# Layer 0 of a four-layer graph network: from one scatter and one sum to four parts with a running maximum

## The chip, the cores and the metric

The kernel runs on one core of one Trainium2 chip. The metric is the device time of one execution in microseconds (us). A core has five engines that run their own instruction queues and meet at semaphores: PE (matrix products), DVE (vector), ACT (scalar functions), POOL (GpSimd) and SP (it issues transfers here). PEld is PE's weight load, "SPq" the sequencer of SP.

## The reference, cut to what matters

Four graph layers run one after the other on 6250 nodes with 128 features and 100000 edges. Each takes the layer-normalized nodes and adds its result to `x`. Only layer 0 is touched:

```python
h = jnp.maximum(_layernorm(x, axis=-1), 0.0)
# layer 0
h = h @ W_w + W_b
e = h[row] @ a_src + h[col] @ a_dst + a_b
e = jax.nn.leaky_relu(e, negative_slope=0.01)
attention = jax.nn.softmax(e, axis=0)            # over all edges
out = jax.ops.segment_sum(attention * h[col], row, num_segments=6250)
x = x + out
```

The softmax runs over all edges at once, so it needs one maximum and one sum over 100000 values; the segment sum goes by the source node `row`.

## The kernel before, in words

`tile_gnn_stack` first prepares tables that all layers share: for instance the masks `mk_d` in device memory that say, for chunks of edges in order of their target, which edge belongs to which node. It counts how many edges have their source in each of the 49 tiles of 128 nodes (`pc`, `cnt`, L209 to L224). Together with other tests on the edge list this makes a flag; where every tile has at most `CAP` = 2304 edges, and at least `FEW` = 1792 (the last tile 1408), the program takes the fast path.

`attention_sum` (L1083) is layer 0 on that path. Its stages run one after the other:

- **Clear.** `rows_d` in device memory has 2304 rows of 130 numbers for each node tile: a message of 128 numbers, the edge's logit and the edge's source node within its tile. L1105 writes, in two transfers, a neutral row (logit -BIG) into each place from `FEW` up, which a scatter may leave empty.
- **Node table.** `ln_relu` and `transposed` make the normalized nodes and their transpose. A loop over 49 tiles of nodes multiplies by the layer's weights (L1152), adds the bias on DVE (`ev`, four buffers, L1154), stores the tile to the table `T0` with a transfer of SP (L1155) and keeps the source part of the logit in `s_tab` (L1156).
- **Scatter.** A loop over `CH` = 196 chunks of 512 edges. `load` brings masks and node windows for four chunks (SP, three buffers). `look_up(k)` builds one-hot matrices on DVE (L1190 to L1194) and lets PE count each edge's place among its tile's rows (L1198 to L1202), look up the source part of the logit (L1208) and the target node's row (`ph`, L1212). `send(k-1)` picks the place (`sel`, `got`, `pos`, L1223 to L1228), copies the row to `rw` on ACT (L1231, six buffers), adds logit and source (L1233 to L1242), and POOL issues four scatters of 128 rows of 520 bytes (L1161).
- **Sum.** Each of 49 reads brings 2304 rows of a node tile (L1265, 18 rows for each partition); every read waits for all scatters. The maximum and the sum of the exponentials go over the partitions on POOL (L1279, L1284). `total(b)` makes, 18 times for each tile, a one-hot matrix weighted with the exponentials on DVE (`oq`, L1294) and a product on PE (L1296). `next_tables(b)` adds to `x`, takes the next layer's norm (`layer_norm`, L1070 to L1078, with Sqrt on ACT beside the Exp of `total`), transposes, multiplies by layer 1's weights and stores the table `T1` (L1310).

Layer 1 (`mean_layer`) then begins: POOL gathers rows of `T1` (L266) and so needs all of it.

A scheduler sets the order of the instructions within each engine's queue from the program and its dependences; the program's order is a wish. In the queues of the kernel before, SP issues the clear, the small loads, 49 stores of `T0` and then the first mask loads.

Of the kernel before, what the change touches and what calls it, by code (L numbers as in the profile page):

```python
# [17 lines left out]
P = 128  # L18
# [21 lines left out]
CAP = 2304  # L40
FEW = (1792, 1408)
RW = D + 2

# [39 lines left out]
def tile_gnn_stack(ctx: ExitStack, tc: tile.TileContext, a: dict, out: bass.AP):  # L83
# [33 lines left out]
    with ExitStack() as st:  # L117
# [30 lines left out]
        ext = one.tile([P, 6], F32, name="ext")  # L148
# [57 lines left out]
        cp = one.tile([P, 8, NT], F32, name="cp")  # L206
        pc = ps.tile([P, 8, NT], F32, name="pc", bufs=1)
        for g in range(TC // 8):
            oh = work.tile([P, 8, NT], BF, name="oh")  # L209
            V.tensor_tensor(oh, iof[:, None, :NT].to_broadcast([P, 8, NT]),  # L210
                            hi[:, 8 * g:8 * g + 8][:, :, None].to_broadcast([P, 8, NT]),
                            OP.is_equal)
            nc.tensor.matmul(pc, ones_b, oh, start=g == 0, stop=g == TC // 8 - 1)
        V.tensor_copy(cp, pc)
        cnt = one.tile([P, NT], F32, name="cnt")
        V.tensor_reduce(cnt, cp.rearrange("p j b -> p b j"), AX.X, OP.add)
        V.tensor_reduce(ext[:, 4:5], cnt, AX.X, OP.max)
        V.tensor_scalar(ext[:, 4:5], ext[:, 4:5], float(CAP), None, op0=OP.is_gt)
        V.tensor_reduce(ext[:, 5:6], cnt[:, :NT - 1], AX.X, OP.min)
        V.tensor_scalar(ext[:, 5:6], ext[:, 5:6], float(FEW[0]), None, op0=OP.is_lt)  # L220
        V.tensor_scalar(cnt[:, NT - 1:], cnt[:, NT - 1:], float(FEW[1]), None, op0=OP.is_lt)
        V.tensor_tensor(ext[:, 5:6], ext[:, 5:6], cnt[:, NT - 1:], OP.add)
# [5 lines left out]
    far = nc.values_load(flag[0:1, 0:1], min_val=0, max_val=7 * P)  # L228
# [854 lines left out]
def attention_sum(ctx, tc, a, x, hT, T1, sh, ln_relu, transposed, bcast_row):  # L1083
# [13 lines left out]
    rows_d = dram.tile([NT * CAP, RW], F32, name="rows_d")  # L1097
    T0 = dram.tile([NP, D + 1], F32, name="T0")

    none = one.tile([P, 7, RW], F32, name="none")  # L1100
    V.memset(none, 0.0)
    V.memset(none[:, :, D:D + 1], -BIG)
    for b0, nb, few in ((0, NT - 1, FEW[0]), (NT - 1, 1, FEW[1])):
        n = (CAP - few) // P
        nc.sync.dma_start(bass.AP(tensor=rows_d.tensor, offset=rows_d.offset + (b0 * CAP + few) * RW,  # L1105
                                  ap=[[n * RW, P], [CAP * RW, nb], [1, n * RW]]),
                          none[:, None, :n, :].rearrange("p o n f -> p o (n f)")
                          .to_broadcast([P, nb, n * RW]))
    sloE = one.tile([P, TC], F32, name="sloE")
    shiE = one.tile([P, TC], F32, name="shiE")  # L1110
    tile_of(nc, one, srcE, shiE)
    lo = one.tile([P, TC], I32, name="lo")
    V.tensor_scalar(lo, srcE, P - 1, None, op0=OP.bitwise_and)
    V.tensor_copy(sloE, lo)
    eE = one.tile([P, TC], F32, name="eE")
    V.memset(eE[:, TR:], -BIG)
# [6 lines left out]
    base = one.tile([P, NT], F32, name="base")  # L1123
    V.memset(base, 0.0)
    nc.gpsimd.iota(base[0:1, :], pattern=[[CAP, NT]], base=0, channel_multiplier=0,
                   allow_small_or_imprecise_dtypes=True)
# [31 lines left out]
    members = []  # L1158

    def scatter(idx, src):  # L1160
        ins = nc.gpsimd.indirect_dma_start(  # L1161
            out=rows_d, out_offset=bass.IndirectOffsetOnAxis(ap=idx, axis=0), in_=src,
            in_offset=None)
        tc.declare_no_dep(ins.ins, group="rows", reason="each edge has a row of its own")
        tc.add_to_no_dep_group("rows", ins.ins)
        members.append(ins)

    with ExitStack() as se:
        w = se.enter_context(tc.tile_pool(name="s0w", bufs=3))
        gp = se.enter_context(tc.tile_pool(name="s0g", bufs=4))  # L1170
        ps = se.enter_context(tc.tile_pool(name="s0p", bufs=2, space=PSUM))
        masks, live = {}, {}
# [9 lines left out]
        def look_up(k):  # L1182


            c0 = 2 if k == 0 else 0
            n = 4 - c0
            t = 4 * k - 2
            dwr, slr, wr = masks.pop(k)
            oh = w.tile([P, 512], F32, name="oh")
            V.tensor_scalar(oh[:, c0 * P:], dwr[:, c0 * P:], pid, None, op0=OP.is_equal)  # L1190
            ol = w.tile([P, 512], F32, name="ol")
            V.tensor_scalar(ol[:, c0 * P:], slr[:, c0 * P:], pid, None, op0=OP.is_equal)
            ob = w.tile([P, 4, NT], BF, name="ob")
            V.tensor_tensor(ob[:, c0:, :], iof[:, None, :NT].to_broadcast([P, n, NT]),  # L1194
                            shiE[:, t + c0:t + 4][:, :, None].to_broadcast([P, n, NT]),
                            OP.is_equal)
            pq = ps.tile([P, 2, 4, NT], F32, name="pq")
            nc.tensor.matmul(pq[:, 0, c0:, :], ones, base[:, None, :].to_broadcast([P, n, NT]),  # L1198
                             start=True, stop=False)
            nc.tensor.matmul(pq[:, 0, c0:, :], tri, ob[:, c0:, :], start=False, stop=False)  # L1200
            for d in range(1, n):
                nc.tensor.matmul(pq[:, 0, c0 + d:, :], ones_b, ob[:, c0:4 - d, :], start=False,  # L1202
                                 stop=d == n - 1)
            up = w.tile([P, NT], F32, name="up")
            V.tensor_reduce(up, ob[:, c0:, :].rearrange("p c b -> p b c"), AX.X, OP.add)
            V.tensor_tensor(base, base, up, OP.add)
            for c in range(c0, 4):
                nc.tensor.matmul(pq[:, 1, c, :], ol[:, c * P:(c + 1) * P], s_tab, start=True,  # L1208
                                 stop=True)
            ph = ps.tile([P, 2, 512], F32, name="ph")  # L1210
            for c in range(c0, 4):
                nc.tensor.matmul(ph[:, c // 2, (c % 2) * (D + 1):(c % 2 + 1) * (D + 1)],  # L1212
                                 oh[:, c * P:(c + 1) * P], wr, start=True, stop=True)
            live[k] = ob, pq, ph

        def send(k):
# [26 lines left out]
            for c in range(c0, 4):  # L1243
                scatter(pos[:, c:c + 1], rw[:, c, :])

        for g in range(2):
            load(g)
        for k in range(CH + 1):
            g, j = divmod(k, SUP)
            if j == 0 and g + 2 < CH // SUP:  # L1250
                load(g + 2)
            if k < CH:
                look_up(k)
            if k > 0:
                send(k - 1)

    w = ctx.enter_context(tc.tile_pool(name="s0x", bufs=3))
    ps = ctx.enter_context(tc.tile_pool(name="s0y", bufs=2, space=PSUM))
    info = mybir.DependencyInfo(mybir.DependencyClass.Sync, mybir.DependencyReason.DATA)
    J = CAP // P  # L1260
    rows, sums = {}, {}

    def read(b):
        t = w.tile([P, J, RW], F32, name="rows", bufs=4)
        ins = nc.sync.dma_start(  # L1265
            t.rearrange("p j f -> p (j f)"),
            bass.AP(tensor=rows_d.tensor, offset=rows_d.offset + b * CAP * RW,
                    ap=[[J * RW, P], [1, J * RW]]))
        for m in members:
            tc.add_manual_dep(ins.ins, m.ins.name, info, reason="reads the scattered rows")  # L1270
        rows[b] = t

    for b in range(3):
        read(b)

    mx = one.tile([P, 1], F32, name="mx")
    V.tensor_reduce(mx, eE, AX.X, OP.max)
    nmx = one.tile([P, 1], F32, name="nmx")
    nc.gpsimd.partition_all_reduce(nmx, mx, P, bass.bass_isa.ReduceOp.max)  # L1279
    V.tensor_scalar(nmx, nmx, -1.0, None, op0=OP.mult)  # L1280
    rs = one.tile([P, 1], F32, name="rs")
    sm = one.tile([P, 1], F32, name="sm")
    S.activation(eE, eE, AF.Exp, bias=nmx, scale=1.0, accum_out=sm)
    nc.gpsimd.partition_all_reduce(rs, sm, P, bass.bass_isa.ReduceOp.add)  # L1284
    V.reciprocal(rs, rs)

    def total(b):
        rb = rows.pop(b)
        ew = w.tile([P, J], F32, name="ew")
        S.activation(ew, rb[:, :, D], AF.Exp, bias=nmx, scale=1.0)  # L1290
        oq = w.tile([P, J, P], F32, name="oq", bufs=2)
        acc = ps.tile([P, D], F32, name="acc")
        for j in range(J):
            V.tensor_scalar(oq[:, j, :], iof, rb[:, j, D + 1:D + 2], ew[:, j:j + 1],  # L1294
                            op0=OP.is_equal, op1=OP.mult)
            nc.tensor.matmul(acc, oq[:, j, :], rb[:, j, :D], start=j == 0, stop=j == J - 1)  # L1296
        sums[b] = acc

    def next_tables(b):
        n = slice(b * P, (b + 1) * P)  # L1300
        V.scalar_tensor_tensor(x[:, b, :], sums.pop(b), rs, x[:, b, :], op0=OP.mult, op1=OP.add)
        h = layer_norm(nc, w, x[:, b, :], eps)
        pt = ps.tile([P, P], F32, name="pt")
        nc.tensor.transpose(pt, h, ident)
        S.copy(hT[:, 0, n], pt)
        pp = ps.tile([P, D], F32, name="pp")
        nc.tensor.matmul(pp, hT[:, 0, n], wa, start=True, stop=True)
        ev = w.tile([P, D], F32, name="ev")
        V.tensor_tensor(ev, pp, b1a, OP.add)
        nc.sync.dma_start(T1[n, :], ev)  # L1310

    for b in range(NT + 1):
        if b + 3 < NT:
            read(b + 3)
        if b < NT:
            total(b)
        if b > 0:
            next_tables(b - 1)
# [808 lines left out]
```

## Time and profile before

| what | us |
|---|---|
| median of three runs (7927.75, 7914.5, 7914.88) | 7914.88 |
| profiled execution: its time / its span | 7935.46 / 7933.7 |
| start to the clear's issue (L1105) | 79.85 |
| node table: first L1154 to last L1156 | 133.2 to 169.0 |
| first scatter (L1161) / end of the last | 182.69 / 1193.91 |
| first gather of layer 1 (L266) | 1492.46 |
| mean granted clock of PE, as a share of full | 0.889 |

Layer 0 with the shared preparation thus takes the first 1492 us of 7934; what follows is not touched. The lines of a group name the source line, the engine, the operation, its tiles, and how often; then busy time and mean duration in ns; then the idle time of the engine just before, and what ended it.

### The profile page before, as it was taken

What the parts mean: (1) busy time and instruction counts of PE and PEld (TensorE: products, weight loads), DVE (VectorE), ACT (ScalarE), POOL (GpSimd) and SP (SyncE); (2) the same over time, 40 slices, a digit from 0 to 9 for tenths busy, and PEclk for the clock granted to TensorE, in tenths of its full rate; (3) what the DMA queues carried; (4) which work ended last, traced back from release to release, by engine and by line L of the source; (5) the groups of instructions that cost most, each with busy time, mean ns of one, the idle gap of its engine ahead of it and who ended that gap; (6) DMA issues with size and microseconds to landing.
All of it is one profiled execution on the core that took longest, in us unless ns stands there. A gap on an engine that the chain in (4) does not pass through costs nothing.

```text
span 7933.7 us, 108436 instructions
## 1 busy us (share of the span) xinstructions
PE 6282.7 (79%) x35210; PEld 4479.0 (56%) x35210; DVE 5018.4 (63%) x16251; ACT 1891.1 (24%) x3935; POOL 5451.0 (69%) x5486
## 2 busy tenths in 40 slices
PE   6776768877876999998777777788878888787787
PEld 3776758655654666665444544555545555555555
DVE  7665658644444999998566667555555555555555
ACT  1111116422222322223111114222222222222222
POOL 0777770377775777773777773777767777677776
PEclk8767669999998999999888887999989999899999
DMA  4433336433334444442333333444434444333333
GB/s 143 120 117 119 112 93 224 139 93 93 92 93 99 142 137 132 136 134 85 94 89 89 88 91 94 125 126 124 125 113 125 121 125 125 113 118 119 117 115 108
DMA packets 734675, 921.89 MB, mean 116 GB/s; under 512 B 230728, under 2 KB 519533, under 8 KB 727605
## 3 DMA queue, kind: packets, MB, share of 16 engines
q1 hardware_dynamic: 518084, 490.05, 20.9%
q0 software_dynamic: 187680, 411.54, 17.9%
q10 hardware_dynamic: 28336, 13.26, 0.6%
q8 instruction: 285, 4.67, 0.2%
q14 instruction: 290, 2.37, 0.1%
HBM read 800.07 MB, written 114.32 MB: 115 GB/s over the span
## 4 chain that ended last, share of the span: by engine, by line
PE 27%; DMA 19%; POOL 12%; issue 7%; DVE 3%; ACT 1%; SPq 0%; POOLq 0%; DVEq 0%; ACTq 0%
DMA gb<-TB,srcE 12%; POOL gb L266 7%; POOL gl L266 5%; PE pa L1770 4%; DMA gl<-TLb,srcE 4%; PE pz L2022 4%; PE pa L2049 3%; PE pm L1656 3%; PE pt L2010 3%; DMA gl<-TL,srcE 2%; PE pb L2035 2%; PE pm L1658 2%; PE pt L2012 2%; PE sp L1680 1%; DVE px L1757 0%
## 5 line engine op out<-in xcount | busy, mean ns | idle before, releaser
L266 POOL DMA_INDIRECT gb<-TB,srcE x2346 | 2247.6, 958 | 863.6 <-issue 548.9
L2024 DVE TENSOR_TENSOR_SCAN sc<-mk,sc,pz 128x512 f32<-128x512 bf16 x585 | 748.5, 1279 | 1125.6 <-PE pz L2022 1125.4
L266 POOL DMA_INDIRECT g<-T,srcE x782 | 743.6, 951 | 528.3 <-DVE oe L1407 290.3
L266 POOL DMA_INDIRECT gl<-TL,srcE x782 | 897.2, 1147 | 280.7 <-issue 157.2
L266 POOL DMA_INDIRECT gl<-TLb,srcE x782 | 790.1, 1010 | 355.3 <-issue 191.1
L1161 POOL DMA_INDIRECT rows_d<-rw,pos x782 | 770.4, 985 | 341.4 <-issue 182.6
L2012 PE MATMUL pt<-ident,gb 128*128 128x128 f32 x2346 | 486.9, 295 | 604.5 <-DMA gb<-TB,srcE 596.5
L2012 PEld LDWEIGHTS pt<-ident,gb 128*128 128x128 f32 x2346 | 314.9, 142 | 1046.8 <-DMA gb<-TB,srcE 768.7
L2015 ACT ACTIVATE z<-pt 128x512 f32<-128x512 f32 (+1 forms) x588 | 350.4, 596 | 1671.8 <-PE pt L2012 1557.8
L1658 PEld LDWEIGHTS pm<-ident,gl 128*128 128x128 f32 x2346 | 321.3, 149 | 683.9 <-DMA gl<-TLb,srcE 325.0
L1656 PE MATMUL pm<-oh,wr 128*128 128x512 f32 (+1 forms) x1176 | 665.1, 650 | 34.6 <-DMA oh<-in_edge_weight 27.7
L1658 PE MATMUL pm<-ident,gl 128*128 128x128 f32 x2346 | 451.7, 294 | 284.2 <-DMA gl<-TLb,srcE 240.9
L2022 PE MATMUL pz<-z,wo 128*128 128x512 f32 (+1 forms) x1176 | 674.5, 658 | 0.0
L2049 PE MATMUL pa<-en,row 128*128 128x128 f32 x4692 | 669.4, 289 | 0.0
L1661 ACT COPY mT<-pm 128x512 f32<-128x512 f32 (+1 forms) x588 | 343.8, 585 | 1297.9 <-PE pm L1658 1172.2
L2049 PEld LDWEIGHTS pa<-en,row 128*128 128x128 f32 x4692 | 624.6, 207 | 0.1
L2010 PE MATMUL pt<-oh,wr 128*128 128x512 f32 (+1 forms) x1176 | 612.4, 603 | 0.5 <-DVE ev L1916 0.5
L1662 DVE SCALAR_TENSOR_TENSOR lT<-mT,pm 128x512 f32<-128x512 f32 (+1 forms) x588 | 389.4, 676 | 319.7 <-ACT mT L1661 318.3
L2041 DVE TENSOR_SCALAR en<-iof,endE 128x128 f32<-128x128 f32 x2346 | 547.4, 300 | 0.0
L1212 PE MATMUL ph<-wr,oh 128*128 128x129 f32 x1564 | 317.7, 369 | 268.8 <-ACT rw L1231 227.3
L2035 PEld LDWEIGHTS pb<-ident,sc 128*128 128x128 f32 x2346 | 325.5, 154 | 359.9 <-issue 358.2
L2037 ACT COPY row<-pb 128x512 f32<-128x512 f32 (+1 forms) x588 | 343.6, 584 | 513.7 <-PE pb L2035 513.0
(317 smaller groups left out, 11842.0 us busy)
## 6 DMA issues: line engine op xcount, KB each, us to landing
mk<-mk_d SPq DMA_DIRECT2D x192, 1024.0 KB
rows<-rows_d SPq DMA_DIRECT2D x49, 1170.0 KB
mk<-mk_d SPq DMA_DIRECT2D x96, 512.0 KB
gb<-TB,srcE POOLq DMA_INDIRECT x2346
wr<-TA SPq DMA_DIRECT2D x141, 256.0 KB
ea<-in_edge_attr SPq DMA_DIRECT2D x195, 128.0 KB
wr<-TR SPq DMA_DIRECT2D x47, 448.0 KB
rows_d<-rw,pos POOLq DMA_INDIRECT x782
```

The costliest lines, as they stand in the source:

```text
L266: nc.gpsimd.indirect_dma_start(out=dst, out_offset=None, in_=table, in_offset=bass.IndirectOffsetOnAxis(ap=idx, axis=0),)
L1161: ins = nc.gpsimd.indirect_dma_start(out=rows_d, out_offset=bass.IndirectOffsetOnAxis(ap=idx, axis=0), in_=src, in_offset=None)
L1656: nc.tensor.matmul(pm[:, c0 * P:], wr[:, fb], oh[:, c0 * P:], start=True, stop=False)
L1658: nc.tensor.matmul(pm[:, c * P:(c + 1) * P], gl[:, c, fb], ident, start=False, stop=c == 3, is_transpose=True)
L1662: V.scalar_tensor_tensor(lT[:, b, c0 * P:], mT[:, c0 * P:], 0.2, pm[:, c0 * P:], op0=OP.mult, op1=OP.max)
L2010: nc.tensor.matmul(pt[:, c0 * P:], wr, oh[:, c0 * P:], start=True, stop=False)
L2012: nc.tensor.matmul(pt[:, c * P:(c + 1) * P], gb[:, c, :], ident, start=False, stop=c == 3, is_transpose=True)
L2022: nc.tensor.matmul(pz[:, c0:], wo[conv], z[:, c0:], start=True, stop=True)
L2024: V.tensor_tensor_scan(sc[:, c0:], masks.pop(k)[1][:, c0:], pz[:, c0:], 0.0 if carry[0] is None else carry[0][:, 511:512], OP.add, OP.max)
L2035: nc.tensor.transpose(pb[:, c, :], sc[:, c * P:(c + 1) * P], ident)
L2041: V.tensor_scalar(en[:, c, :], iof, endE[:, t:t + 1], None, op0=OP.is_equal)
L2049: nc.tensor.matmul(pa, row[:, c, :], en[:, c, :], start=c == c0, stop=c == 3)
```

## The change

The chunks are cut into four parts at chunks 58, 114 and 160 (`SEG`). Each part has its own `rows_d`, with room for 768, 768, 640 and 512 rows in a node tile (6, 6, 5 and 4 for each partition, 21 together; 18 before), its own clear and its own counts in the test that chooses the fast path. In the edge list here a node tile has at most 641, 647, 530 and 413 edges in parts 0 to 3, and at least 549, 513, 434 and 332 (the last tile 488, 515, 402 and 409), all within the limits.

While part s+1 is scattered, part s is summed by `sum_part`, a generator that is advanced by one or two node tiles in a chunk: `peak` takes the part's maximum (with the one before it) through two small PE steps, `fetch` reads a node tile's rows, `weigh` multiplies the rows by the exponentials on ACT, one row of a partition at a time (`wt`), and makes all one-hot matrices of the tile in one DVE instruction (`oq`), which reads the node numbers from PSUM (`bank[:, 2]`). PE sums into `bank`, and `keep` brings the sum to `acc` on DVE, where an earlier sum is scaled by the exponential of the change of the maximum (`scl`). After the loop only part 3 is left. There the reads come in groups of seven node tiles, the Exp and the Sqrt are taken once for each group, and the steps of the norm, the transpose and the next table are spread over the following tiles.

`clear(0)` stands where the clear was. The clears 1 to 3 are written in the chunk loop, at chunks 8, 20 and 32.

The diff, cut to its core:

```diff
-CAP = 2304
-FEW = (1792, 1408)
+SEG = (0, 58, 114, 160, 196)
+CAP = (768, 768, 640, 512)
+FEW = ((384, 384), (384, 256), (256, 256), (256, 256))
+def seg_tiles(s):
+
+    return max(4 * SEG[s] - 2, 0), 4 * SEG[s + 1] - 2
...
+        for s in range(len(CAP)):
+            t0, t1 = seg_tiles(s)
...
+            V.tensor_reduce(cnt, pc.rearrange("p j b -> p b j"), AX.X, OP.add)
+            x0 = 4 + 3 * s
...
+
+    def clear(s):
+        for b0, nb, few in ((0, NT - 1, FEW[s][0]), (NT - 1, 1, FEW[s][1])):
+            n = (CAP[s] - few) // P
+            nc.sync.dma_start(bass.AP(tensor=rows_d[s].tensor,
+                                      offset=rows_d[s].offset + (b0 * CAP[s] + few) * RW,
+                                      ap=[[n * RW, P], [CAP[s] * RW, nb], [1, n * RW]]),
+                              none[:, None, :n, :].rearrange("p o n f -> p o (n f)")
+                              .to_broadcast([P, nb, n * RW]))
+
+    clear(0)
...
+    def part_of(k):
+        return max(s for s in parts if SEG[s] <= k)
+
+    def scatter(s, idx, src):
         ins = nc.gpsimd.indirect_dma_start(
-            out=rows_d, out_offset=bass.IndirectOffsetOnAxis(ap=idx, axis=0), in_=src,
+            out=rows_d[s], out_offset=bass.IndirectOffsetOnAxis(ap=idx, axis=0), in_=src,
             in_offset=None)
-        tc.declare_no_dep(ins.ins, group="rows", reason="each edge has a row of its own")
-        tc.add_to_no_dep_group("rows", ins.ins)
-        members.append(ins)
+        tc.declare_no_dep(ins.ins, group=f"rows{s}", reason="each edge has a row of its own")
+        tc.add_to_no_dep_group(f"rows{s}", ins.ins)
+        members[s].append(ins)
+    def read(s, t, b, n):
+
+        J = CAP[s] // P
+        ins = nc.sync.dma_start(
+            t, bass.AP(tensor=rows_d[s].tensor, offset=rows_d[s].offset + b * CAP[s] * RW,
+                       ap=[[J * RW, P], [CAP[s] * RW, n], [1, J * RW]]))
+        for m in members[s]:
+            tc.add_manual_dep(ins.ins, m.ins.name, info, reason="reads the scattered rows")
+    def peak(s, w, pm):
+
+        e = eE[:, slice(*seg_tiles(s))]
+        mx = w.tile([P, 1], F32, name="mx")
+        V.tensor_reduce(mx, e, AX.X, OP.max)
+        if s > 0:
+            V.tensor_tensor(mx, mx, top[:, s - 1:s], OP.max)
+        nc.tensor.transpose(pm[0:1, :P], mx, ident)
+        m1 = w.tile([1, 1], F32, name="m1")
+        V.tensor_reduce(m1, pm[0:1, :P], AX.X, OP.max)
+        nc.tensor.matmul(pm[:, P:P + 1], ones[0:1, :], m1, start=True, stop=True)
+        V.tensor_copy(top[:, s:s + 1], pm[:, P:P + 1])
+        V.tensor_scalar(ntop[:, s:s + 1], top[:, s:s + 1], -1.0, None, op0=OP.mult)
+        sm = w.tile([P, 1], F32, name="sm")
+        S.activation(e, e, AF.Exp, bias=ntop[:, s:s + 1], scale=1.0, accum_out=sm)
+        if s == 0:
+            V.tensor_copy(sums[:, 0:1], sm)
+        else:
+            S.activation(scl[:, s:s + 1], top[:, s - 1:s], AF.Exp, bias=ntop[:, s:s + 1], scale=1.0)
+            V.scalar_tensor_tensor(sums[:, s:s + 1], sums[:, s - 1:s], scl[:, s:s + 1], sm,
+                                   op0=OP.mult, op1=OP.add)
+
+    def weigh(w, rb, ew, J, row, bufs):
+
+        wt = w.tile([P, J, D], F32, name=f"wt{J}", bufs=bufs)
+        for j in range(J):
+            S.activation(wt[:, j, :], rb[:, j, :D], AF.Copy, scale=ew[:, j:j + 1])
+        oq = w.tile([P, J, P], F32, name=f"oq{J}", bufs=bufs)
+        V.tensor_tensor(oq, row[:, None, :].to_broadcast([P, J, P]),
+                        rb[:, :, D + 1:D + 2].to_broadcast([P, J, P]), OP.is_equal)
+        return wt, oq
...
+        bank = p1.tile([P, 3, P], F32, name="bank")
+        V.tensor_copy(bank[:, 2, :], iof)
+        pm = p1.tile([P, P + 1], F32, name="pm")
...
-                scatter(pos[:, c:c + 1], rw[:, c, :])
+                scatter(part_of(k), pos[:, c:c + 1], rw[:, c, :])
+        def sum_part(s):
+
+            J = CAP[s] // P
+            rows, mats = {}, {}
+
+            def fetch(b):
+                rows[b] = w.tile([P, J, RW], F32, name=f"rows{J}", bufs=4)
+                read(s, rows[b].rearrange("p j f -> p (j f)")[:, None, :], b, 1)
+
+            def prepare(b):
+                rb = rows.pop(b)
+                ew = w.tile([P, J], F32, name=f"ew{J}")
+                S.activation(ew, rb[:, :, D], AF.Exp, bias=ntop[:, s:s + 1], scale=1.0)
+                mats[b] = weigh(w, rb, ew, J, bank[:, 2, :], 2)
+
+            def add_up(b):
+                wt, oq = mats.pop(b)
+                for j in range(J):
+                    nc.tensor.matmul(bank[:, b % 2, :], oq[:, j, :], wt[:, j, :], start=j == 0,
+                                     stop=j == J - 1)
+
+            def keep(b):
+                if s == 0:
+                    V.tensor_copy(acc[:, b, :], bank[:, b % 2, :])
+                else:
+                    V.scalar_tensor_tensor(acc[:, b, :], acc[:, b, :], scl[:, s:s + 1],
+                                           bank[:, b % 2, :], op0=OP.mult, op1=OP.add)
+
+            peak(s, w, pm)
+            for b in range(3):
+                fetch(b)
+            yield
+            for b in range(NT + 2):
+                if b + 3 < NT:
+                    fetch(b + 3)
+                if b >= 2:
+                    keep(b - 2)
+                if b >= 1 and b - 1 < NT:
+                    add_up(b - 1)
+                if b < NT:
+                    prepare(b)
+                yield
 
...
         for k in range(CH + 1):
             g, j = divmod(k, SUP)
             if j == 0 and g + 2 < CH // SUP:
                 load(g + 2)
+            if k in (8, 20, 32):
+                clear((k - 8) // 12 + 1)
             if k < CH:
                 look_up(k)
             if k > 0:
                 send(k - 1)
-
+            for s in parts[:-1]:
+
+                n = SEG[s + 2] - SEG[s + 1] - 4
+                i = k - SEG[s + 1] - 2
+                if i == 0:
+                    work = sum_part(s)
+                if 0 <= i < n:
+                    for _ in range((i + 1) * (NT + 3) // n - i * (NT + 3) // n):
+                        next(work)
...
+    def fetch(g):
+        t = w.tile([P, 7, J * RW], F32, name="rows")
+        read(s, t, 7 * g, 7)
+        groups[g] = t.rearrange("p b (j f) -> p b j f", j=J)
+
+    for g in range(2):
+        fetch(g)
...
     def total(b):
-        rb = rows.pop(b)
-        ew = w.tile([P, J], F32, name="ew")
-        S.activation(ew, rb[:, :, D], AF.Exp, bias=nmx, scale=1.0)
-        oq = w.tile([P, J, P], F32, name="oq", bufs=2)
-        acc = ps.tile([P, D], F32, name="acc")
+        g, i = divmod(b, 7)
+        ew, mv = accs[g]
+        wt, oq = weigh(w, groups[g][:, i, :, :], ew[:, i, :], J, bank[:, P + 8:], 2)
+        pa = ps.tile([P, D], F32, name="pa")
         for j in range(J):
-            V.tensor_scalar(oq[:, j, :], iof, rb[:, j, D + 1:D + 2], ew[:, j:j + 1],
-                            op0=OP.is_equal, op1=OP.mult)
-            nc.tensor.matmul(acc, oq[:, j, :], rb[:, j, :D], start=j == 0, stop=j == J - 1)
+            nc.tensor.matmul(pa, oq[:, j, :], wt[:, j, :], start=j == 0, stop=j == J - 1)
+        normed[b] = pa
...
+    def weights(g):
+        ew = w.tile([P, 7, J], F32, name="ew")
+        S.activation(ew, groups[g][:, :, :, D], AF.Exp, bias=ntop[:, s:s + 1], scale=1.0)
+        mv = w.tile([P, 7, 2], F32, name="mv")
+        accs[g] = ew, mv
+    def add(b):
+        g, i = divmod(b, 7)
+        V.scalar_tensor_tensor(acc[:, b, :], acc[:, b, :], scl[:, s:s + 1], normed.pop(b),
+                               op0=OP.mult, op1=OP.add)
+        V.scalar_tensor_tensor(x[:, b, :], acc[:, b, :], rs, x[:, b, :], op0=OP.mult, op1=OP.add)
+        st = w.tile([P, 6], F32, name="lnst")
...
+    def scales(g):
+        mv = accs.pop(g)[1]
+        groups.pop(g)
+        r = w.tile([P, 7, 2], F32, name="lnrs")
+        S.activation(r[:, :, 0], mv[:, :, 1], AF.Sqrt, bias=eps, scale=1.0)
+        V.reciprocal(r[:, :, 0], r[:, :, 0])
+        V.scalar_tensor_tensor(r[:, :, 1], mv[:, :, 0], -1.0, r[:, :, 0], op0=OP.mult, op1=OP.mult)
+        accs[g] = r
...
-    for b in range(NT + 1):
-        if b + 3 < NT:
-            read(b + 3)
+    for b in range(NT + 11):
+        g, i = divmod(b, 7)
+        if i == 0 and g < 7:
+            if g + 2 < 7:
+                fetch(g + 2)
+            weights(g)
+        if 0 <= b - 1 < NT:
+            add(b - 1)
         if b < NT:
             total(b)
-        if b > 0:
-            next_tables(b - 1)
+        if i == 0 and 1 <= g <= 7:
+            scales(g - 1)
+        if 0 <= b - 10 < NT:
+            table(b - 10)
+        if 0 <= b - 9 < NT:
+            turn(b - 9)
+        if 0 <= b - 8 < NT:
+            norm(b - 8)
```

## The prediction

> **What bounds layer 0 now.** The groups of the page come first. Of the lines of layer 0 one stands among the costliest:
>
> ```profile
> L1161 POOL DMA_INDIRECT rows_d<-rw,pos x782 | 770.4, 985 | 341.4 <-issue 182.6
> ```
>
> A scatter takes 0.985 us on POOL. The waits between 200 and 1190 us, inside the chunk loop, say who sets its pace:
>
> ```profile
> ACT rw L1231 <- DMA rows_d<-rw,pos: 592.7, 110, 9.8
> PEld ph L1212 <- ACT rw L1231: 282.7, 67, 7.5
> DVE pos L1228 <- issue: 216.8, 46, 6.4
> ...
> POOL rows_d L1161 <- issue: 179.9, 590, 0.3
> ```
>
> POOL waits 0.3 us 590 times for nothing but its own issue; ACT waits for buffers that scatters must free, PE waits for ACT. So POOL bounds the loop: 1011 us from first to last scatter for 782 of them, 5.06 us for a chunk of four. The other engines by stretch (busy us and instructions of PE, PEld, DVE, ACT, POOL; then the clock granted to PE, the DMA share, GB/s):
>
> ```profile
> 133.00:169.00 36.00, 31.93 (x99) 23.47 (x99) 22.46 (x104) 0.00 (x0) 0.00 (x0) 0.50 0.32 89
> 300.00:310.00 10.00, 10.00 (x48) 9.85 (x49) 7.85 (x30) 1.17 (x2) 7.78 (x8) 0.50 0.16 53
> 600.00:800.00 200.00, 133.81 (x839) 126.56 (x838) 120.88 (x462) 22.89 (x39) 152.91 (x155) 0.74 0.40 118
> 1250.00:1400.00 150.00, 139.97 (x1007) 130.34 (x1007) 143.38 (x621) 101.20 (x156) 0.00 (x0) 1.00 0.62 218
> ```
>
> The 155 scatters of the third row are 38.75 chunks: 3.45 us of PE a chunk at clock 0.74, 2.55 at full clock, 3.12 of DVE, 0.59 of ACT. So there is room beside POOL's 5.06. In the sum stage (last row) POOL does nothing; DVE is busy 96%, PE 93%. Its groups, 1196 to 1492 us:
>
> ```profile
> L1296 PE MATMUL acc<-rows,oq 128*128 128x128 f32 x1764 | 254.5, 296 | 60.7 <-DMA rows<-rows_d 43.6 <-DVE oq L1294 17.0
> L1294 DVE TENSOR_SCALAR oq<-iof,rows,ew 128x128 f32<-128x128 f32 x882 | 242.8, 340 | 0.6 <-DVE rs L1285 0.6
> ...
> L1074 ACT ACT_TABLE_LOAD x45 | 57.7, 1283 | 0.8
> L1290 ACT ACT_TABLE_LOAD x44 | 56.5, 1283 | 16.1 <-DMA rows<-rows_d 9.0 <-DVE oq L1294 5.4 <-DVE ev L1309 0.9
> L1078 ACT ACTIVATE lnh<-x,lnrs 128x128 f32<-128x128 f32 x49 | 24.1, 493 | 47.5 <-DVE lnrs L1076 47.5
> ```
>
> The stage lasts 298.5 us, from the last scatter's end at 1193.91 to layer 1's first gather at 1492.46. What the change puts in front of the loop meets the node table's loop and the clear. The tile `ev` and the DMA rate of 78 to 130 us in 40 slices show both:
>
> ```profile
> L1155 SPq DMA_DIRECT2D T<-ev x49: 319/320/1460, 133.5 to 168.5; - x49
> GB/s 0 95 342 293 290 290 296 291 287 293 369 381 381 384 381 382 384 381 384 381 381 381 379 384 384 379 381 382 382 382 381 384 381 384 381 386 351 75 71 52
> ```
>
> The stores leave 0.72 us apart; the clear runs at 382 GB/s.
>
> **The tail (gain).** After the loop only part 3 is left: 4 instead of 18 rows per partition.
> - PE, 36 to 8 passes a tile: at 254.5/1764 = 0.144 us, 1.15, with transpose and table product (3 passes) about 1.6 us.
> - DVE: one `oq` of 512 elements, priced by `sel` (392 elements, also from PSUM, 0.561 us) at 0.65; `acc`, `x` 0.35 each by L1301, norm 0.285 + 0.175, `ev` 0.29: about 2.1.
> - ACT: four weighted copies. No row has that form; it lies between the 128x128 copy from PSUM (L1305, 0.265 us) and L1078 with two pointers (0.493). I take 0.29, as a copy with one pointer is nearer to the copy. With 0.46 for the norm (its start-to-start), 0.27 for the copy and (2 x 1.28 + 0.33 + 0.30)/7 = 0.46 for table loads, Exp and Sqrt of a group, it is 2.35 summed; starts overlap the ends before them by some 5%, so 2.25.
>
> ACT is the longest: 49 x 2.25 = 110. In front come 1.8 us to the read's issue and 1.86 MB at 418 GB/s (spacing of the old reads, 1170 KB in 2.86 us) with 2.2 of latency: 8.5. Behind it about 3 for the last tile's chain and the 3.1 us that separate the last `ev` from the first gather now. Sum 126, against 298.5: **-172** (ACT copies at 0.265 and 0.46 give -182 and -136).
>
> **Before the loop (loss).** The order of instructions in the changed kernel's queues shows what the diff hides: the scheduler draws clears 1 to 3 forward from chunks 8, 20 and 32 into the node table's loop, on SP, after 24, 32 and 38 of its 49 stores. Each later store waits in that queue; `ev` has four buffers, so DVE stops four tiles on, `s_tab` stays incomplete, and `look_up(0)` stands behind it on DVE and PE. The clears move 9.58, 9.58 and 6.39 MB, with tails 26.2 MB: 68 us at 382 GB/s. Their pieces are 1560 and 1040 bytes, against 2080 in the old clear, so a fixed share per piece may add some 5. Landing between clears and stores costs about 2 us each, and some 10 us of tile work hide under them: **+70**. Against it: clear 0 is 9.8 instead of 13.2 MB (-9, of which DVE's wait of 6.3 us for `av`, queued behind it, can give -6), the first mask loads now stand before the stores (-3.4, DVE's wait at L1190), and the count has three more final reduces of some 1.4 us (L216 to L221; +4). Sum **+65**. Bounds: 55, if more tiles hide; 105, if a clear costs 6144 pieces whatever their size (33.5 us, the old clear at its rate).
>
> **In the loop.** Part 0 is summed at one tile a chunk (52 steps in 52 chunks), part 1 at 1.24 (42), part 2 at 1.63 (32, five rows).
> - PE gets 12 or 10 passes a tile, 1.73 or 1.44 us at full clock: 2.55 becomes 4.28, 4.70 and 4.90 us a chunk, under 5.06.
> - DVE: `oq` of 768 elements, along the line from `ob` (196 elements, 0.352) to `sel`, 0.96; of 640, 0.83; `keep` 0.29 and 0.35. 3.12 becomes 4.4, 4.7, 5.0.
> - ACT: six copies and an Exp, about 2.1 a tile: 2.7 to 3.6.
> - Reads of 0.4 MB a chunk take 1 us of DMA at a share of 0.40 now: covered.
>
> At a part's start `fetch` waits for the part's last scatter (1.8 us) and its landing (3.2). DVE stands at `oq` behind row chunk 59, ACT behind 61; POOL then has two finished chunks, 10 us, against some 7.5 until the next: covered, though by 2.5 us only. `bank` is one PSUM buffer that DVE reads while PE writes, so `oq`, `add_up` and `keep` take turns; this and a DVE load of 98% will not always fit in 5.06. I put 0.2 us on each of 126 chunks: **+24** (0 to 70).
>
> What decides here is PE's clock: at 0.74 the chunks take 5.8, 6.35 and 6.6 us, which costs 38 + 54 + 49 = 141 us. The second row shows PE busy throughout at 0.50, the fourth 93% busy at 1.00. I expect mostly the latter, since the sums fill the pauses in which it cools now (PE waits up to 7.2 us for `rw`).
>
> The Trainium skill ("TensorE: Matmul & The Clock Gate", Part 1, "What's actually happening") says that about 3.4 us of sustained work release the full clock. By that rule the 141 fall away entirely. The trace agrees only in part: 10 us of unbroken work stayed at 0.50.
>
> **Sum.** -172 + 65 + 24 = -83. The profiled execution had 7935.5 us; its sum is 7852. The median of the runs, 7914.9, is 20.6 lower: **7832 us**.
>
> **Rivals.**
> 1. *PE stays throttled* (slower). The turns at `bank` break PE's work often enough that it stays near 0.74, as the node table's loop stayed at 0.50 while 89% busy. Then -172 + 65 + 141 = +34: 7949. It is slower from 107 us of loop loss on, 5.91 us a chunk, which is clock 0.78 at the mean need of 4.58. For it: rows one to three. Against it: the sum stage, with the same small products, at 1.00. Chance 0.16.
> 2. *The clears do not hold up the stores* (land beside the node table). Then before the loop -5, in all -153: 7762. Against it: one queue, and 382 GB/s is all that a clear got. Chance 0.10.
> 3. *Each clear costs the old one's time whatever its size, and ACT's copies 0.46.* -136 + 100 + 24 = -12: 7903. Chance 0.10.
> 4. *The change doesn't do what it says*: the fast path isn't taken. The counts of edges exclude that; 0.01.
>
> **How the numbers follow.** The forecast keeps 0.63, with its own range 7780 to 7890: tail by 15 either way, clears -10 to +25, loop -24 to +40, not all at once. The whole range, 7765 to 7905, leaves out rival 1, the lower half of rival 2, and little else. A measurement of this kernel can tell about 0.2%, 16 us. Slower by more: rival 1 with a bit of 3, 0.16. Same: the edge between 1 and 3, 0.05. Faster: 0.79.
>
> **What would show it.** Right: last L1180 store near 240 us instead of 168.5, with the stores bunched behind `rows_d<-none`; the first scatter near 247; 1030 to 1040 us to the last one; PE's clock over 0.9 between 500 and 1200; about 126 us to layer 1's gather, ACT the busiest there. Wrong: first scatter near 180 (rival 2), scatters 6 us or more a chunk apart with the clock under 0.8 (rival 1), a pause of POOL over 5 us at chunks 62, 118 and 164 (the cover at a part's start missing), or a tail over 150 us.

## The result, and the profile after

The changed kernel takes 7816.09 us (median of four runs, 7813.23 to 7816.58) against 7914.69 for the kernel before: ratio 0.9872, 95% interval 0.9855 to 0.9889. It is 98.6 us faster; 83 were forecast, as 7832 us. (A fourth run of the kernel before, 7909.88, moves its median from 7914.88 to 7914.69.)

| stretch | before | after | change | forecast |
|---|---|---|---|---|
| start to the first scatter | 182.69 | 253.08 | +70.4 | +65 |
| first scatter to the end of the last | 1011.2 | 1015.9 | +4.7 | +24 |
| from there to layer 1's first gather | 298.5 | 121.1 | -177.5 | -172 |
| sum | | | -102.4 | -83 |

The spans of the two profiled executions differ by 122.3 us. The 20 that the table lacks lie behind layer 0, in code that is the same; the profiled execution of before stood 20.8 above its median.

Before the loop, SP's queue (start, duration, line, transfer, how many):

```profile
151.60 1.98 SPq L1180 DMA_DIRECT2D T<-ev  x4
153.64 0.42 SPq L1119 DMA_DIRECT2D rows_d<-none  x1
154.22 24.36 SPq L1180 DMA_DIRECT2D T<-ev  x4
178.63 1.24 SPq L1119 DMA_DIRECT2D rows_d<-none  x1
184.34 1.98 SPq L1180 DMA_DIRECT2D T<-ev  x4
186.38 0.43 SPq L1119 DMA_DIRECT2D rows_d<-none  x1
186.90 24.66 SPq L1180 DMA_DIRECT2D T<-ev  x4
...
218.27 18.17 SPq L1180 DMA_DIRECT2D T<-ev  x4
```

The large transfer of each clear goes out in under half a microsecond; the four stores behind it hold SP for the 24.4, 24.7 and 18.2 us in which it lands. DVE pays for it, as the idle time ahead of the tile `ev` says (us, times):

```profile
  DMA T<-ev: 87.9, 14
```

In the kernel before it was 8.2 us:

```profile
  DMA T<-ev: 8.2, 21
```

In the loop, the waits between 260 and 1265 us, and then three stretches (busy us and instructions of PE, PEld, DVE, ACT, POOL; granted clock, DMA share, GB/s): no sums, part 0, part 1.

```profile
ACT rw L1306 <- DMA rows_d<-rw,pos: 273.3, 59, 9.2
POOL rows_d L1189 <- issue: 168.9, 554, 0.3
...
ACT wt L1231 <- PE bank L1339: 53.9, 56, 2.3
```

```profile
400.00:450.00 50.00, 30.28 (x191) 28.39 (x192) 27.77 (x108) 5.87 (x10) 38.11 (x40) 0.75 0.44 133
600.00:650.00 50.00, 47.86 (x379) 43.58 (x378) 46.78 (x162) 28.20 (x88) 38.41 (x39) 0.97 0.72 219
900.00:950.00 50.00, 48.14 (x399) 44.55 (x399) 48.41 (x159) 33.64 (x108) 38.11 (x40) 1.00 0.76 231
```

POOL still waits 0.3 us at most scatters, and it issues 39 or 40 in 50 us with and without sums. PE fills up to 96% and DVE to 97%, and PE's clock rises from 0.75 to 1.00 in the same step.

How far the preparation is ahead of POOL can be read from the traces: this lead is the time from the last write of a chunk's `rw` and `pos` to its first scatter. In the kernel before it stays between 17.4 and 22.9 us from chunk 12 on. In the changed kernel it falls to 3.3, 3.6 and 2.3 us at chunks 62, 118 and 164, where a part's sums begin (the least is 1.5, at chunk 117), and comes back to 18 us or more before the next part. The scatters themselves are a little longer, 0.994 us on the mean (0.985 before):

```profile
L1189 POOL DMA_INDIRECT rows_d<-rw,pos x782 | 777.6, 994 | 407.4 <-DVE sel L1298 170.8
```

The tail, 1269 to 1396 us:

```profile
L1231 ACT ACTIVATE wt<-rows,ew 128x128 f32<-128x128 f32 x196 | 62.2, 393 | 0.9 <-PE pa L1419 0.6
...
L1233 DVE TENSOR_TENSOR oq<-bank,rows 128x512 f32<-128x512 f32 x49 | 33.0, 676 | 2.9 <-DMA rows<-rows_d 2.9
...
L1435 ACT ACT_TABLE_LOAD x5 | 6.4, 1283 | 0.1
L1409 ACT ACT_TABLE_LOAD x4 | 5.1, 1283 | 0.1
```

```profile
1285.00:1375.00 90.00, 75.66 (x467) 68.41 (x468) 72.89 (x271) 87.59 (x272) 0.00 (x0) 0.89 0.36 118
```

89 table loads have become 9, and ACT is the bound at 97%.

### The profile page after: what moved, and what is told of

Read it like the earlier page. It is cut to its first block, busy times and chain, and to the rows that moved or that the text cites. A ratio compares the mean times of both kernels' runs of the same rounds, so it can differ in the third digit from the quotient of the medians.

```text
span 7811.4 us, 110134 instructions
## 1 busy us (share of the span) xinstructions
PE 6179.0 (79%) x35518; PEld 4376.7 (56%) x35518; DVE 4978.6 (64%) x15715; ACT 2093.4 (27%) x4956; POOL 5446.3 (70%) x5487
## 3 DMA queue, kind: packets, MB, share of 16 engines
q0 software_dynamic: 187680, 411.54, 18.2%
## 4 chain that ended last, share of the span: by engine, by line
PE 27%; DMA 19%; POOL 12%; issue 7%; DVE 3%; ACT 0%; SPq 0%; POOLq 0%; DVEq 0%; ACTq 0%
DMA gb<-TB,srcE 12%; POOL gb L277 7%; POOL gl L277 5%; DMA gl<-TLb,srcE 4%; PE pz L2183 4%; PE pa L1931 4%; PE pa L2210 4%; PE pm L1817 3%; PE pt L2171 3%; DMA gl<-TL,srcE 2%; PE pb L2196 2%; PE pm L1819 2%; PE pt L2173 2%; PE sp L1841 1%; DVE px L1918 1%
## 5 line engine op out<-in xcount | busy, mean ns | idle before, releaser
L1599 DVE TENSOR_TENSOR y<-y,pa 64x129 f32<-64x129 f32 (+3 forms) x388 | 111.9, 288 | 460.6 <-PE pa L1588 455.0
```

## The experiments

Times of a stretch are read from the trace of each run; ratios are to the kernel before on the same chip.

**Clears kept in the loop.** `info` and `members` come from the changed kernel.

```diff
-    def clear(s):
+    def clear(s, after=None):
...
+            if after is not None:
+                tc.add_manual_dep(ins.ins, after.ins.name, info, reason="not before the loop")
...
-                clear((k - 8) // 12 + 1)
+                clear((k - 8) // 12 + 1, members[0][-1])
```

> The changed kernel, with clears 1 to 3 made to wait for the last scatter issued before chunks 8, 20 and 32, so that they can't be drawn forward among the stores of the node table. Theory (the clears delay the first scatter because the stores stand behind them in one queue): first scatter at 180 to 185 us instead of 253, loop within 10 us of its 1016, tail unchanged: 7740 to 7755. Rival (their 26 MB cost the same wherever they stand, because scatters and mask loads inside the loop then land later): the loop grows by 50 to 70 us, 7805 to 7820.

Measured 7753.5 us, ratio 0.9781 (0.9765 to 0.9798). First scatter at 183.44, 69.6 us earlier; loop 1014.6; tail 121.7.

```profile
219.07 31.15 SPq L1119 DMA_DIRECT2D rows_d<-none  x2
```

```profile
230.00:255.00 25.00, 17.48 (x94) 16.51 (x95) 15.33 (x58) 2.93 (x5) 19.20 (x20) 0.64 1.08 280
```

Clear 1 now holds SP for 31 us and fills the DMA engines (share 1.08; packets count where they start, so it can pass 1), and POOL still issues 20 scatters in 25 us. The theory holds: all that the clears cost was their place in the queue. The same 26 MB are free in the loop: while they land the lead of the preparation falls to 5.2 us (chunk 20), and not to nothing. This one change undoes nearly the whole loss of 70.

**The node numbers in SBUF.**

```diff
-                mats[b] = weigh(w, rb, ew, J, bank[:, 2, :], 2)
+                mats[b] = weigh(w, rb, ew, J, iof, 2)
```

> The changed kernel, but the one-hot matrices of parts 0 to 2 compare with the node numbers in SBUF instead of in the PSUM buffer that PE writes. Theory 1 (the loop is paced by POOL, and the turns of DVE and PE at that buffer are hidden): within 8 us of 7816, loop 1010 to 1020 us. Theory 2 (the turns cost what the loop lost, as the prediction's 0.2 us a chunk had it): 3 to 5 us faster, since the loop lost 5. Rival (the Trainium skill, SBUF - State Buffer, Who interferes with whom: a two-input vector instruction with both inputs in SBUF contends with a GpSimd instruction that reads SBUF): the mean scatter rises from 0.994 us; one scatter delayed by up to 0.9 us for each of 147 tiles would be up to 130 us, and in part hidden 30 to 130: 7846 to 7946.

Measured 7857.91, ratio 0.9913 (0.9896 to 0.9929): slower than the changed kernel, with intervals apart. The loop takes 1038.3 us, 22.5 more. (The ratios differ by some 32 us; 6 of the rest stand before the loop, and the next run, on the same chip and without this edit, has 5 of them too.) Groups of 250 to 1320 us of this run:

```profile
L1189 POOL DMA_INDIRECT rows_d<-rw,pos x782 | 800.2, 1023 | 413.4 <-DVE ob L1269 179.5 <-issue 172.5 <-ACT wt L1231 13.4
...
L1233 DVE TENSOR_TENSOR oq<-iof,rows 128x768 f32<-128x768 f32 x98 | 93.1, 950 | 30.5 <-DMA rows<-rows_d 30.5
```

`oq` itself takes 0.95 us as before (0.956) and waits no longer for PE, but the mean scatter goes from 0.994 to 1.023 us: 29 ns x 782 = 23 us, the loop's growth. So the wait at `bank` was hidden (theory 1 against 2 in the loop), and the rival came: reading one operand from PSUM is what keeps the sums from slowing POOL. The trace shows it at single scatters. Two that begin 0.47 us after an `oq`, first in the changed kernel, then in this run:

```profile
643.31 0.96 DVE L1233 TENSOR_TENSOR oq<-bank,rows 128x768 f32<-128x768 f32 x1 [1.18 <-PE bank L1339]
643.78 0.96 POOL L1189 DMA_INDIRECT rows_d<-rw,pos  x1 [0.30 <-issue]
```

```profile
609.85 0.95 DVE L1233 TENSOR_TENSOR oq<-iof,rows 128x768 f32<-128x768 f32 x1
610.32 1.31 POOL L1189 DMA_INDIRECT rows_d<-rw,pos  x1 [0.30 <-issue]
```

In the changed kernel 75 scatters begin within 0.6 us of the start of an `oq`; all take 0.954 to 0.962 us. In this run there are 68; they take 1.384 on the mean, and 62 of them end 0.83 to 0.85 us after the end of their `oq`, whenever they began: they are held until it is done. The Trainium skill ("SBUF — State Buffer", "Who interferes with whom") says that a vector instruction with two inputs from SBUF contends with a GpSimd instruction that reads SBUF. The trace agrees. The expectation's upper bound of 130 us took one delay for each of 147 tiles; 23 were measured, as fewer scatters begin at such a time and the delay is only what is left of the `oq`.

**Tables for each tile.** In the tail, `weights` and `scales` act on one tile, not on seven:

```diff
+        S.activation(ew[:, i, :], groups[g][:, i, :, D], AF.Exp, bias=ntop[:, s:s + 1], scale=1.0)
...
+        S.activation(r[:, i, 0:1], mv[:, i, 1:2], AF.Sqrt, bias=eps, scale=1.0)
...
-        if i == 0 and 1 <= g <= 7:
-            scales(g - 1)
+        if 0 <= b - 2 < NT:
+            scales(b - 2)
```

> The changed kernel, but in the tail the Exp and the Sqrt are taken for each node tile by itself, as in the kernel before, not for groups of seven. Theory (ACT bounds the tail at 1.96 us a tile): 98 table loads instead of 9 add 89 x 1.283 = 114 us, and 84 more short activations some 25: the tail grows from 121 to about 250 us, 7930 to 7960. Rival (the loads hide beside DVE and PE, as 89 of them seemed to in the kernel before): tail under 150 us, 7816 to 7845.

Measured 7946.7, ratio 1.0035 (1.0021 to 1.0049): slower than the kernel before. The tail takes 246.9 us.

```profile
1290.00:1490.00 200.00, 107.05 (x436) 91.39 (x437) 89.35 (x326) 197.54 (x404) 0.00 (x0) 0.51 0.15 50
```

ACT is busy 99%. Its 89 loads (80 more than in the changed kernel, 98 were expected) are 103 of the 126 us, the short Exp and Sqrt most of the rest. Without the grouping the change, as it is written, would have lost.

**The grouping alone, in the kernel before.** `next_tables` is replaced by the changed kernel's `add`, `scales`, `norm`, `turn` and `table`; the sums, with 18 rows a partition, stay.

> The kernel before, with one change of the tail alone: Sqrt for groups of seven node tiles and the steps of the norm spread over the following tiles, so that the table loads of the sum stage fall from 89 to 15 (95 us of ACT less). Still one part and 18 rows a partition. Theory (DVE at 96% bounds that stage, 18 one-hot products at 0.27 us each): 0 to 10 us faster, 7905 to 7915; so the change's gain comes from the rows summed inside the loop. Rival (the loads stood on the path): 60 to 95 us faster, 7820 to 7855.

Measured 7917.35, ratio 0.9991 (0.9981 to 1.0). The sum stage takes 290.7 us, 7.8 less.

```profile
1250.00:1400.00 150.00, 145.09 (x1052) 134.78 (x1051) 146.18 (x599) 35.04 (x91) 0.00 (x0) 1.00 0.66 227
```

ACT falls from 101 to 35 us in this stretch, DVE stays the bound (97%; PE is as full). The loads, now 13, were off the path as long as 18 one-hot products stood on it. With the run before: the halves of the tail's change give -8 alone (the grouping) and -52 (fewer rows, from 298.5 to 246.9), and both together -177.

**Denser sums.**

```diff
-                n = SEG[s + 2] - SEG[s + 1] - 4
+                n = (SEG[s + 2] - SEG[s + 1] - 4) // 2
```

> The changed kernel, but each part is summed in half as many chunks: two node tiles a chunk in part 0, 2.5 in part 1, 3.25 in part 2. By the prices of the prediction a chunk then needs 6.0, 6.8 and 7.2 us of PE at full clock, against 5.2 that POOL takes: a deficit of 21, 35 and 33 us in 26, 21 and 16 chunks, of which some 20 us each are covered by the four to six chunks that are prepared ahead. Theory (the loop was free because every engine stayed under POOL's pace): the loop grows by 20 to 60 us. Rival (the sums cost nothing because they fill pauses whatever their density): within 8 us of the changed kernel.

Measured 7824.9, ratio 0.9886 (0.987 to 0.9903). The loop takes 1023.9, 8.1 more than the changed kernel's: at the rival's edge, under the theory's 20. Twice the density costs next to nothing. The lead shows how near the edge it is: it falls to 0.8 us at chunk 62, stays between 0.7 and 1.9 to chunk 89, and is over 20 again at chunk 98. So the start of a part takes nearly all of the cover and the sparse chunks behind give it back; in between the preparation keeps POOL's pace, where by the prices (6.0 us of PE a chunk) it should have fallen behind. The prices were too high. Where it is spent: POOL's longest idle times inside the loop are 3.3, 1.6 and 1.9 us at the starts of the three parts (574, 862 and 1100 us), and some dozen of 0.7 us behind ACT; in the changed kernel none is over 0.5.

**Toward a better version.** On top of the clears in the loop: POOL weighs one of four rows in the tail; the node numbers get a PSUM buffer of their own (beside `pm`), read by `oq` and by `ob`, the 128x196 one-hot of each chunk; and both.

```diff
+            if j in pool:
+                nc.gpsimd.tensor_scalar(wt[:, j, :], rb[:, j, :D], ew[:, j:j + 1], None, op0=OP.mult)
```

```diff
+        pm = p1.tile([P, 2 * P + 8], F32, name="pm")
+        row = pm[:, P + 8:]
+        V.tensor_copy(row, iof)
```

> The kernel with the clears kept in the loop, and in the tail POOL, which is idle there, weighs one of the four rows of a partition in place of ACT. (The form is used in the loop's sums by ACT alone as before.) Theory (ACT bounds the tail at 1.96 us a tile, DVE needs 1.65 and PE 1.7): ACT falls by 0.32 a tile, the tail from 121 to about 107 us, 10 to 15 us faster than with the clears in the loop alone, ratio 0.9762 to 0.977. Rival (POOL and the two-input DVE instructions hold each other up): no gain or slower, ratio 0.978 and above.

> The kernel with the clears kept in the loop; the node numbers stand in a PSUM buffer that PE writes three times only, and both one-hot instructions of the loop (the one of the sums and the 128x196 of every chunk, which read both inputs from SBUF until now) read them there. Theory (a two-input DVE instruction with both inputs in SBUF lengthens the scatters that run beside it, as the run with the row in SBUF showed: 0.994 to 1.023 us): the mean scatter falls from 0.991 to 0.965 to 0.98 us, the loop by 8 to 20 us, ratio 0.9755 to 0.977. Rival (only the long 768-element form does it): 0.99 us and the loop within 4 us, ratio 0.9775 to 0.9785.

> The clears in the loop, POOL weighing a row in the tail, and the node numbers apart, together. If both theories hold the gains add: 20 to 30 us below the clears in the loop alone, ratio 0.974 to 0.9755. If neither: 0.978.

| kernel | us | ratio, interval | loop | mean scatter | tail |
|---|---|---|---|---|---|
| clears in the loop | 7753.5 | 0.9781 (0.9765 to 0.9798) | 1014.6 | 0.991 | 121.7 |
| POOL weighs | 7743.1 | 0.9783 (0.9767 to 0.98) | 1023.2 | 1.004 | 112.8 |
| numbers apart | 7739.83 | 0.9779 (0.9762 to 0.9795) | 1009.3 | 0.986 | 120.4 |
| both | 7731.28 | 0.9768 (0.9752 to 0.9785) | 1015.8 | 0.993 | 108.4 |

The first row ran on a chip where the kernel before takes 7923.06, the others where it takes 7912.38; so ratios are compared. POOL's help is real in the tail, 9 us of the 14 expected:

```profile
L1234 POOL TENSOR_SCALAR wt<-rows,ew 128x128 f32<-128x128 f32 x49 | 29.5, 602 | 67.6 <-PE pa L1424 43.6 <-ACT ew L1414 9.5 <-PE pt L1451 7.0
```

In that run the loop, whose code is the same, took 9 us more, and by the ratio the rival's forecast came true: no gain. The loss goes with the edit. In all four runs in which POOL weighs (two here, two below) the shortest scatter takes 0.963 to 0.965 us and the median one 0.969; in the ten other traces it is 0.952 to 0.955 and 0.958 to 0.962. Eleven ns on 782 scatters are 8.6 us, what the tail gained; why each scatter grows isn't shown. The numbers apart bring 5 us in the loop, between theory and rival, and nothing that the ratios can tell. Both together are the fastest kernel on the usual chips, 7731.28 us, though its interval overlaps that of the clears alone, and the 0.974 to 0.9755 of gains that add was missed.

**A smaller tail.** Part 2 ends at chunk 164, part 3 keeps three rows a partition (at most 370 edges a node tile): once on top of all the above, once on the clears in the loop alone.

```diff
-SEG = (0, 58, 114, 160, 196)
-CAP = (768, 768, 640, 512)
+SEG = (0, 58, 114, 164, 196)
+CAP = (768, 768, 640, 384)
```

And in the kernel before, with `row` a PSUM copy of `iof`:

```diff
-            V.tensor_tensor(ob[:, c0:, :], iof[:, None, :NT].to_broadcast([P, n, NT]),
+            V.tensor_tensor(ob[:, c0:, :], row[:, None, :NT].to_broadcast([P, n, NT]),
```

> As the run with POOL weighing and the node numbers apart (ratio 0.9768), but part 2 ends at chunk 164 instead of 160, and part 3 has room for 384 rows a node tile, three a partition. ACT then has 1.3 us a tile in the tail, DVE about 1.5, PE 1.45. Theory (the tail follows the busiest engine): tail 98 to 103 us instead of 108; the sums of part 2, now in 28 instead of 32 chunks, stay under cover: ratio 0.975 to 0.9765. Rival (the tail is no longer bound by an engine but by the chain from tile to tile): tail 106 and above, ratio 0.9765 to 0.978.

> The clears kept in the loop, and part 3 with three rows a partition from chunk 164 on; no work on POOL and the node numbers where the change has them. Theory (ACT bounds the tail, a weighted copy costs 0.32 us from start to start): the tail falls from 121 to 105 or 108 us, 13 to 16 us faster than with the clears in the loop alone: ratio 0.976 to 0.9768. Rival (rows count little, the norm's chain does): tail above 115, ratio 0.9775 and above.

> The kernel before, with one change: the one-hot of node tiles in each chunk (128x196, L1194) reads the node numbers from PSUM instead of SBUF. Theory (a two-input DVE instruction with both inputs in SBUF lengthens the scatters beside it, by its 0.35 us in one chunk or another): the mean scatter falls from 0.985 to 0.96 to 0.975 us, the loop by 8 to 20 us: ratio 0.9975 to 0.999. Rival (other DVE instructions lengthen them, such as one-input forms, and this one not): 0.98 us and more, ratio 0.9995 to 1.0005.

> The same kernel as the last but two (clears in the loop, POOL weighing one row in the tail, node numbers apart, three rows a partition in part 3), on a chip where the kernel before takes its usual 7.9 ms. Theory (each saving stands in a stage of its own and they add): before the loop -70, loop within 10 us, tail 104 us instead of 121: 7720 to 7735, ratio 0.9745 to 0.977. Rival (the loop gives the saving back, since the sums of part 2 have fewer chunks): ratio 0.9775 and above.

These four ran on chips where the kernel before takes 9384.86 (the last: 9329.39) us, so their ratios stand apart from the others: 0.9858 (0.9835 to 0.988), 0.9874 (0.9853 to 0.9895), 1.0012 (0.9997 to 1.0028), and 0.9833 (0.9811 to 0.9854) for the first kernel again. There POOL is held up at single scatters without any of this change, too; the third of these runs (the kernel before with `row` in PSUM), between 601 and 609 us:

```profile
601.29 0.95 POOL L1161 DMA_INDIRECT rows_d<-rw,pos  x1 [0.30 <-issue]
608.73 0.95 POOL L1161 DMA_INDIRECT rows_d<-rw,pos  x1 [6.48 <-issue]
```

Its loop takes 1291 us, not 1011; the sum stage, 298.7 us, is as on the other chips, so the tails can be compared. They are 103.7, 103.6 (first kernel, two runs) and 107.4 us. The last is 14.2 under the 121.7 of four rows, within the theory's 13 to 16: ACT's weighted copies set the tail. With POOL's help and three rows it is 103.7 where 98 to 103 were expected; the first kernel's stretch shows DVE at 88% and ACT at 87%, so no single engine is the bound there:

```profile
1540.00:1610.00 70.00, 54.77 (x351) 45.76 (x352) 61.86 (x253) 61.23 (x175) 25.18 (x41) 0.95 0.41 126
```

The forecast that the last kernel would reach 7720 to 7735 us could not be decided: no run of it fell on a usual chip.

With `row` in PSUM the kernel before is no faster by the ratio, as that rival had it (mean scatter 0.977 us against 0.985, on different chips). The traces say what happened. In the kernel before, 34 scatters begin in the first 0.2 us of an `ob` and take 1.085 to 1.187 us; with its node numbers in PSUM there are 36 (42 in the run with the numbers apart), and all take 0.954 to 0.962. So `ob` does hold scatters up, and PSUM ends it. But those that begin in the first 0.35 us of `oh`, which DVE makes two steps earlier from one tensor, go from 1.092 (51) to 1.185 (55): most of the delay now stands there. Why is not shown.

## Why the prediction was right

- **The tail, -172, measured -177.5.** The step holds: ACT is the bound, from its first Exp at 1277.88 to the end of its last copy at 1384.57, 2.18 us a tile where 2.25 was put; 8.9 us stand in front (8.5 forecast) and 5.4 behind (6.1). The run with tables for each tile shows the mechanism. The weighted copy's price is 0.294 us from start to start (mean of 196), as estimated; with three rows ACT's stretch is 11 us shorter, 0.23 a tile.
- **Before the loop, +65, measured +70.4.** Clears in the store queue, shown by putting them elsewhere (-69.6). Three parts: the node table starts at 129.2 instead of 133.2 (-4.0, forecast -2); from its first to its last `ev` it takes 114.4 instead of 35.0 (+79.4, forecast +70); the first scatter then follows after 9.5 instead of 14.5 (-5.0, forecast -3.4). The middle one was too small: also with the clears in the loop the stores took 43.9 us, as they stand 5 us apart in fours at the start, with loads of masks and windows among them. Which of these holds them was not tried.
- **In the loop, +24, measured +4.7.** This is the step that failed: the 0.2 us a chunk stood for turns at `bank` and a full DVE. Both are there (DVE 97% in part 1, ACT waits 53.9 us for PE's `bank`), but they are hidden, as the row in SBUF and the denser sums show. What the loop did lose is in the scatters: 0.994 instead of 0.985 us are 7.2 us, less 2.5 in which POOL waited less. The starts of the parts were covered, as forecast, and as narrowly: the lead is 3.3, 3.6 and 2.3 us there, where 2.5 was put, and POOL never idles over 0.5 us after the first scatter. One reason why there was more room is a slip: 1011 us for 782 scatters are 5.17 us a chunk, not 5.06.
- **Other slips.** The tail's terms add to 125 us, not 126; copies at 0.265 and 0.46 would give about -178 and -142, not -182 and -136; 0.2 us on 126 chunks are 25. None moves the forecast by more than the 16 us that a measurement can tell.
- **Luck.** The misses of the tail (5.5 us too little gain) and before the loop (5.4 too little loss) cancel; that the forecast is 16 us off comes mostly from the loop term.
- **Rival 1, the throttled PE**, did not come: 0.97 and 1.00 where sums run, 0.75 where none do. The mean from 500 to 1200 us is 0.89, a little under the sign's 0.9, as the stretches between the sums count. The reason given (the sums fill the pauses in which PE cools) fits, and the run with denser sums repeats it: 1.00 from 600 to 700 us with sums, 0.66 from 800 to 850 without, 1.00 again from 900 to 1000. A run that breaks PE's work was not made.
- **Rival 2** did not come: the change as written holds up the stores. Its saving is real, though; with the clears out of the stores' way the kernel gives 0.9781.
- **Rival 3** did not come: the clears held the queue 24.4, 24.7 and 18.2 us, not 33.5 each, and a copy took 0.29 us, not 0.46.

## What to carry to other kernels

Look up where a scheduler really puts a bulk transfer: the same 26 MB cost 70 us ahead of small stores in one queue and nothing inside a loop that is bound elsewhere, and one dependence moves it. When the work on one engine is cut, price the next engine's fixed costs: grouping the table loads was worth 8 us before the cut and 126 after it. Beside scatters issued by POOL, give a long vector instruction one of its inputs from PSUM if it costs nothing, and check its neighbours: for the short `ob` it gained nothing that could be told. Read single instructions and not only means: a mean that moved by 29 ns was in the main 62 scatters that were held until another engine was done.

## What the runs showed of the hardware that had not been expected

The same kernel takes 7.91 to 7.92 ms on some chips and 9.33 to 9.38 on two others; there POOL stands up to 6.5 us at single scatters, and the scatter loop takes 1291 us. Whether the chip or the moment makes the difference, no run shows. A clear in pieces of 1040 bytes held the queue 18.2 us for 6.39 MB, in pieces of 1560 bytes 24.5 for 9.58, with as many pieces: bytes count, but on the line through the two points 5.6 us do not go with them. One instruction of another form on POOL, in the tail, went with 11 ns more on every scatter of the loop before it.
